# An adaptive-layernorm block with a gated scan and a routed expert layer: weights loaded apart from rows, early scatters, one more block table, and a bias added by VectorE

## The chip, the cores and the metric

The kernel runs on one core of a Trainium2 chip. Five engines work beside each other, each through its own queue in order: TensorE (PE in the profile, with its weight loads as PEld), VectorE (DVE), ScalarE (ACT), GpSimd (POOL) and SyncE (SP). The metric is the device time of one execution in microseconds; lower is better. The time before is the median of nine runs, 473.71 us.

## The reference

`x` holds 32 sequences of 256 tokens with 128 features, 8192 tokens in all. Cut to what matters:

```python
mod = (silu(c) @ wmod).reshape(32, 6, 1, -1)
sa, ca, ga, sb, cb, gb = (mod[:, i] for i in range(6))
ga = (2 * (ga >= 0) - 1) * maximum(abs(ga), 0.25)       # gb likewise
h = layernorm(x) * (1 + ca) + sa
g, a, v = sigmoid(h @ Wg.T + bg), sigmoid(h @ Wd.T + bd), h @ Wv.T + bv
x = x + ga * g * scan(h_t = a_t * h_{t-1} + (1 - a_t) * v_t)
h = layernorm(x) * (1 + cb) + sb
probs = softmax(h @ gate_w.T + gate_b)                  # 8 experts
gate = probs where among the two largest, else 0
y = relu(h @ w1[e] + b1[e]) @ w2[e] + b2[e]             # for each expert e
x = x + gb * sum_e gate[:, e] * y[:, e]
```

Here `w1[e]` is 128 x 512 and `w2[e]` is 512 x 128. Only the two chosen experts of a token have a weight other than zero, so the kernel computes two pairs (token, expert) for each token.

## The kernel before

**Supertiles.** The 8192 tokens are cut into 16 supertiles (`s`) of 512 tokens, each four tiles of 128. A supertile goes through four steps: `a_norm` (first layernorm), `a_mix` (three products, gates and the scan), `a_res` (residual and second layernorm) and `a_route` (router, ranks, and the rows to send). The string `HEAD` lays out the first six rounds; after it a round does one step of each of four supertiles. The step letters are n, m, r and R.

**Scatter by expert.** `a_route` writes each token's normalised row twice into `rw` (once for each chosen expert), followed by its gate value and the number of the place its result belongs to: `RW = D + 2` words (L69). It finds the row's place within its expert's region by ranks, counted with products against triangular and all-one matrices (L423, L425) and written as indices `pi` (L439). Eight indirect DMAs a supertile, issued by GpSimd, scatter the rows into `reg` in HBM (L447). They aren't issued at once: `drip` (L461) takes one or two of them from the list `sending` after each step and each block, and makes each wait for the last ScalarE instruction of that step or block. The tile `rw` and the indices `pi` have three buffers.

**Blocks.** A block is 256 rows of one expert. How many blocks are full after a supertile depends on the data; what is sure is a lower bound, `full(s)`. At the supertiles in `TAKE` a `table` is computed on VectorE (L471 to L520) that lists expert and place of the next blocks; 45 are listed by the tables up to supertile 12, and the last table, after supertile 15, lists the rest of the 71. Blocks of a table are held back (`held`) until the rows of its supertile have been sent.

**A block's work** is three steps, each in another `b_step`, so that three blocks are in flight:
- `b_load` (L533): SyncE reads expert and place from the table into registers (L535, L536), loads the block's rows `xr` (130 KB, waiting for the sixteen scatters issued last) and then the expert's first weights and bias `ww` (514 KB, five buffers). It runs `LOOK = 4` blocks ahead.
- `b_in` (L547): PE transposes the rows (L551), ScalarE and VectorE split them into a high and a low part (L553, L554).
- `b_up` (L557): twelve products (L566 to L568), then four ReLUs with bias; in the first `HA = 53` blocks one of the four is done by VectorE (L572), the rest by ScalarE (L574).
- `b_down` (L578): PE reads the expert from the table (L581), puts the second bias into the accumulator by a product of ones with the bias's two parts (L584), and adds sixteen products (L587). The accumulator `pby` has one buffer. ScalarE copies it out as `yt`, scaled by the gate value that came with the rows (L591); `yt` has eight buffers (`YTB`). Two indirect DMAs from GpSimd scatter `yt` into `yd`, in the order of tokens (L593).

**Final sums.** When the blocks up to a certain one are done, `c_load` (L600) loads the two results of every token of a supertile into `yk` (two buffers), and `c_add` (L610), up to three supertiles behind (`CLAG`), adds them, multiplies by the row of `gb` that PE spreads over partitions (L614, L621), adds `x` (L622) and stores (L623). The supertiles up to `CUT` are ready together, at a block of the last table.

**Order.** The four steps carry priorities (`AHEAD`), and a scheduler orders each engine's instructions when the kernel is built; within an engine nothing overtakes. All loads and stores of the main part are issued by SyncE, all scatters by GpSimd.

Of the kernel before, what the change touches and what calls it, by code (L numbers as in the profile page):

```python
# [11 lines left out]
I32 = mybir.dt.int32  # L12
# [14 lines left out]

TAKE = (2, 3, 4, 5, 6, 7, 8, 10, 12)
CUT = 9

# [12 lines left out]

HA = 53

# [9 lines left out]
def adaln_moe(ctx: ExitStack, tc: tile.TileContext, x, Wg, bg, Wv, bv, Wd, bd,  # L55
# [12 lines left out]
    NJ = BLK // P  # L68
    RW = D + 2  # L69

# [30 lines left out]
    gbb = cp.tile([P, E], F32, name="gbb")  # L101
    b2r = cp.tile([E, D], F32, name="b2r")
    for s in range(1, XE):
# [6 lines left out]
    nc.gpsimd.dma_start(gbb, gate_b.partition_broadcast(P))  # L110
    nc.gpsimd.dma_start(b2r, b2)
    ones_f = cp.tile([P, P], F32, name="ones_f")
# [4 lines left out]
    nc.gpsimd.affine_select(tri, ones_b, pattern=[[1, P]], compare_op=ALU.is_gt, fill=0.0, base=0, channel_multiplier=-1)  # L117
    ones_r = cp.tile([2, P], F32R, name="ones_r")
    nc.vector.tensor_copy(ones_r, ones_f[0:2, :])

# [92 lines left out]
    wr = cp.tile([P, E, H], F32, name="wr")  # L213
    b2w = cp.tile([K, E, D], F32R, name="b2w")
    b2s = cp.tile([E, 2, D], F32R, name="b2s")
    N3 = 3 * NB
# [3 lines left out]
    def late_constants():  # L220
        nc.vector.tensor_copy(b2s[:, 0], b2r)
        nc.vector.tensor_tensor(b2s[:, 1], b2r, b2s[:, 0], op=ALU.subtract)
        for h in range(2):
            nc.sync.dma_start(b2w[h:h + 1].bitcast(F32), b2s[:, h].bitcast(F32))

# [36 lines left out]
    nc.gpsimd.iota(padi, pattern=[[P, NJ]], base=K * N, channel_multiplier=1)  # L262
    nc.vector.tensor_copy(pad[:, :, D + 1].bitcast(I32), padi)

# [6 lines left out]
    tc.add_to_no_dep_group("fill", f.ins)  # L271

    mh = cp.tile([P, T, 1], F32, name="mh")
    nc.vector.memset(mh, -0.5)
# [110 lines left out]
    def a_route(a, base):  # L385
# [57 lines left out]
        nc.vector.reciprocal(rc, sm)  # L443
        nc.vector.tensor_tensor(rw[:, :, :, D], e8[:, :, 0:K], rc.unsqueeze(2).to_broadcast([P, T, K]), op=ALU.mult)
        nc.gpsimd.tensor_copy(rw[:, :, :, D + 1].bitcast(I32), dst[:, s * T:(s + 1) * T])
        def send(j, k):
# [5 lines left out]

        sending.extend((s, send, j, k) for j in range(T) for k in range(K))
        return rk[:, T]

# [3 lines left out]
    held = []  # L459

    def drip(n, behind):  # L461
        for _ in range(min(n, len(sending))):
            s, send, j, k = sending.pop(0)
            w = send(j, k)
            tc.add_manual_dep(w, behind.ins.name, WAIT, reason="pace of the rows on their way out")
            sent.append(w)
            if not sending or sending[0][0] != s:
                while held and held[0][0] <= s:
                    blocks.extend(held.pop(0)[1])

# [61 lines left out]

    def b_load(n, tb, i):  # L533
        with tc.issue_after(loaded[-1].ins) if loaded else nullcontext():
            e = nc.sync.value_load(tb[i:i + 1, 0:1], min_val=0, max_val=E - 1)  # L535
            r = nc.sync.value_load(tb[i:i + 1, 1:2], min_val=0, max_val=E * CAP)  # L536
        xr = bk.tile([P, NJ, RW], F32, tag="xr", name=f"xr{n}", bufs=YTB + 6)
        w = nc.sync.dma_start(xr, reg[bass.ds(r, BLK)].rearrange("(t p) d -> p t d", p=P))
        tc.add_to_no_dep_group("rows", w.ins)
        for x in sent[-2 * K * T:]:  # L540
            tc.add_manual_dep(w.ins, x.name, WAIT, reason="its rows")
        ww = bk.tile([P, WW], F32, tag="ww", name=f"ww{n}", bufs=5)
        b = dict(n=n, xr=xr, ww=ww, tb=tb, i=i)
        loaded.append(nc.sync.dma_start(ww, wd[bass.ds(e, 1)].rearrange("o p f -> p (o f)")))
        return b

# [10 lines left out]
    def b_up(b):  # L557
        n, xs, ww = b["n"], b["xs"], b["ww"]
        hh = bk.tile([P, NH, BLK], F32, tag="hh", name=f"hh{n}")
        for k0 in range(0, NH, 2):  # L560
# [8 lines left out]
            for k in (k0, k0 + 1):  # L569
                bias = ww[:, O_B1 + k:O_B1 + k + 1]  # L570
                if k % 4 == 1 and n < HA:
                    nc.vector.tensor_scalar(hh[:, k], p1[:, k - k0], bias, 0.0, op0=ALU.add, op1=ALU.max)  # L572
                else:
                    w = nc.scalar.activation(hh[:, k], p1[:, k - k0], AF.Relu, bias=bias)  # L574
                    b.setdefault("last", w)
        b["hh"] = hh

    def b_down(b):  # L578
        n, xr, hh, i = b["n"], b["xr"], b["hh"], b["i"]
        py = psb.tile([P, 512], F32, tag="pby", name=f"pby{n}")[:, :NJ * D]  # L580
        e = nc.tensor.value_load(b["tb"][i:i + 1, 0:1], min_val=0, max_val=E - 1)  # L581
        we = wr[:, bass.ds(e, 1), :].rearrange("p o f -> p (o f)")
        b2t = b2w[:, bass.ds(e, 1), :].to_broadcast([2, NJ, D])
        nc.tensor.matmul(py.rearrange("p (j d) -> p j d", d=D), ones_r, b2t, start=True, stop=False)  # L584
        for j in range(NJ):
            for k in range(NH):
                nc.tensor.matmul(py[:, j * D:(j + 1) * D], hh[:, k, j * P:(j + 1) * P], we[:, k * D:(k + 1) * D],  # L587
                                 start=False, stop=(j == NJ - 1 and k == NH - 1))
        yt = bk.tile([P, NJ, D], F32, tag="yt", name=f"yt{n}", bufs=YTB)
        for j in range(NJ):  # L590
            nc.scalar.activation(yt[:, j], py[:, j * D:(j + 1) * D], AF.Copy, scale=xr[:, j, D:D + 1])  # L591
        for j in range(NJ):
            w = nc.gpsimd.indirect_dma_start(  # L593
                out=yd, out_offset=bass.IndirectOffsetOnAxis(ap=xr[:, j, D + 1:D + 2].bitcast(I32), axis=0),
                in_=yt[:, j], in_offset=None, bounds_check=K * N - 1, oob_is_err=False)
# [14 lines left out]
    def c_add(s, yk, step):  # L610
# [5 lines left out]
        for j0 in range(0, T, step):  # L616
            js = slice(j0, j0 + step)
            nc.vector.tensor_tensor(ot[:, js], yk[:, 0, js], yk[:, 1, js], op=ALU.add)
            for q in range(j0 // JB, (j0 + step) // JB):
# [10 lines left out]
    nload = 0  # L630
    LOOK = 4

    def b_step():

        nonlocal nload
# [48 lines left out]
    for t, todo in enumerate(steps):  # L684
        def step3(s):
            nonlocal base, done
            with tc.high_priority(AHEAD[3] * (s >= EARLY)):
# [11 lines left out]
                elif s == NS - 1:  # L699
# [65 lines left out]
```

## Time and profile before

| | |
|---|---|
| median of nine runs | 473.71 us (472.88 to 478.02) |
| profiled execution | 477.95 us, of which the span from first to last instruction is 476.2 us |
| busy share of the span | PE 86%, weight loads 73%, VectorE 60%, ScalarE 61%, GpSimd 61% |
| mean granted PE clock | 0.913 of full speed |
| scatters of rows (L447) | 128, 981 ns each |
| scatters of results (L593) | 142, 994 ns each |
| bias products (L584) | 71, 384 ns each (pipelined) |
| DMA | 91.5 MB, 192 GB/s over the span |

The span's row is the length between the first and the last instruction of the profiled execution. A line of the windows gives a stretch in us from the start of the span, then the busy time of each engine in it. A line of a timeline gives the start, the duration, the engine, the line of the kernel, the operation, the tile it writes and the tiles it reads, and in brackets how long the engine sat idle before it and what ended that. Matmuls overlap, so that the distance between two starts tells more than a duration.

### The profile page before, as it was taken

The page shows a single profiled execution, that of the slowest core. Times are in us where ns is not written, and L with a number is a line of the kernel's source. Part 1 is how long each engine was busy: PE and PEld are TensorE (multiplying, and loading weights), DVE is VectorE, ACT ScalarE, POOL GpSimd, SP SyncE. Part 2 cuts the span into 40 slices and gives each one's busy share as a digit, 9 for nine tenths or more (in the row PEclk, how much of TensorE's full clock was granted, in tenths as well). Part 3 has the DMA queues.
Part 4 walks back from the last instruction along what each step waited for, and adds up shares of the span by engine and source line. Part 5 has one row for each costly group of instructions (what it writes and reads, how often), then busy time and mean ns, then how long its engine had stood idle before and what let it go on. Part 6 is the DMA issues. An engine that isn't in the chain of part 4 may idle for free.

```text
span 476.2 us, 11399 instructions
## 1 busy us (share of the span) xinstructions
PE 409.7 (86%) x2810; PEld 346.6 (73%) x2810; DVE 285.1 (60%) x1511; ACT 291.4 (61%) x726; POOL 291.5 (61%) x322
## 2 busy tenths in 40 slices
PE   4757665779999999998996999999769999799980
PEld 3224433468988988987886999899669999699970
DVE  6899999968987886883884445122013214444464
ACT  4766654768979877965763666555326566446640
POOL 3633755536777777777677777777754445334551
PEclk9985758779999999998997999999959999889996
DMA  7997211183737656555543767885189869999773
GB/s 194 329 308 252 85 39 40 45 285 88 232 102 229 178 160 206 143 167 140 156 141 104 232 192 211 204 241 166 50 263 274 249 207 289 303 301 330 226 216 112
DMA packets 81845, 91.52 MB, mean 192 GB/s; under 512 B 8577, under 2 KB 66408, under 8 KB 81782
## 3 DMA queue, kind: packets, MB, share of 16 engines
q1 hardware_dynamic: 73024, 73.84, 54.5%
q0 software_dynamic: 8704, 16.94, 10.3%
q8 instruction: 26, 0.43, 0.4%
q14 instruction: 37, 0.30, 0.2%
q10 hardware_dynamic: 54, 0.02, 0.0%
HBM read 64.24 MB, written 27.43 MB: 192 GB/s over the span
## 4 chain that ended last, share of the span: by engine, by line
PE 67%; DVE 12%; DMA 9%; issue 4%; ACT 2%; POOL 2%; SPq 2%; POOLq 0%; ACTq 0%; DVEq 0%
PE pby L587 28%; PE p L566 7%; PE p L567 7%; PE p L568 7%; PE pz L346 5%; PE pby L584 4%; PE pbx L551 3%; DMA yd<-yt,xr 2%; DMA reg<-rw,pi 2%; DVE sta L280 2%; DMA yk<-yd 2%; PE pl L397 2%; DMA ww<-wd 2%; PE po L374 2%; DMA xa<-in_L_attn_x_dram 1%
## 5 line engine op out<-in xcount | busy, mean ns | idle before, releaser
L593 POOL DMA_INDIRECT yd<-yt,xr x142 | 141.1, 994 | 93.0 <-ACT yt L591 55.6
L447 POOL DMA_INDIRECT reg<-rw,pi x128 | 125.6, 981 | 50.3 <-issue 22.5
L587 PE MATMUL pby<-wr,hh 128*128 x1136 | 154.1, 289 | 0.0
L587 PEld LDWEIGHTS pby<-wr,hh 128*128 128x128 f32 x1136 | 139.7, 199 | 9.4 <-issue 0.9
L574 ACT ACTIVATE hh<-p,ww 128x256 f32<-128x256 f32 x231 | 97.8, 476 | 19.8 <-PE p L568 11.9
L591 ACT ACTIVATE yt<-pby,xr 128x128 f32<-128x128 f32 x142 | 45.0, 365 | 84.1 <-PE pby L587 84.0
L566 PE MATMUL p<-xs,ww 128*128 128x256 f32 x284 | 89.2, 315 | 4.5 <-DMA ww<-wd 3.9
L554 DVE TENSOR_TENSOR xs<-pbx,xs 128x256 fp32r<-128x256 f32 x71 | 29.9, 421 | 101.3 <-ACT xs L553 100.8
L568 PE MATMUL p<-xs,ww 128*128 128x256 f32 x284 | 81.6, 288 | 0.0
L567 PE MATMUL p<-xs,ww 128*128 128x256 f32 x284 | 81.4, 287 | 0.0
L346 PE MATMUL pz<-h,wT 128*128 128x512 f32 x96 | 56.2, 704 | 8.9 <-ACT tg L361 3.5
L566 PEld LDWEIGHTS p<-xs,ww 128*128 128x128 f32 x284 | 54.9, 194 | 6.3 <-issue 4.2
L567 PEld LDWEIGHTS p<-xs,ww 128*128 128x128 f32 x284 | 55.3, 195 | 0.7 <-issue 0.7
L568 PEld LDWEIGHTS p<-xs,ww 128*128 128x128 f32 x284 | 55.0, 194 | 0.2 <-issue 0.2
L346 PEld LDWEIGHTS pz<-h,wT 128*128 128x128 f32 x96 | 19.5, 231 | 24.9 <-issue 9.9
L551 PE MATMUL pbx<-ident,xr 128*128 128x128 f32 x142 | 28.4, 283 | 5.9 <-DMA xr<-reg 5.9
L324 ACT ACTIVATE xn<-xa,nra,nya 128x128 f32<-128x128 f32 x64 | 26.4, 489 | 10.1 <-DVE nra L307 10.1
L572 DVE TENSOR_SCALAR hh<-p,ww 128x256 f32<-128x256 f32 x53 | 25.4, 478 | 11.5 <-ACT hh L574 9.5
L553 ACT ACTIVATE xs<-pbx 128x256 fp32r<-128x256 f32 x71 | 27.6, 388 | 7.0 <-PE pbx L551 7.0
L584 PE MATMUL pby<-b2w,ones_r 2*128 x71 | 27.2, 384 | 2.0 <-ACT yt L591 2.0
L402 ACT ACTIVATE rw<-pb 128x1024 f32<-128x1024 f32 x16 | 16.4, 1023 | 19.6 <-DMA reg<-rw,pi 5.9
L382 ACT ACTIVATE xm<-xa,nrb,nyb 128x128 f32<-128x128 f32 x64 | 26.4, 484 | 1.4 <-DVE nrb L307 1.3
(181 smaller groups left out, 574.7 us busy)
## 6 DMA issues: line engine op xcount, KB each, us to landing
ww<-wd SPq DMA_DIRECT2D x71, 514.0 KB
xr<-reg SPq DMA_DIRECT2D x71, 130.0 KB
yk<-yd SPq DMA_DIRECT2D x30, 256.0 KB
wd<-wh SPq DMA_DIRECT2D x8, 514.0 KB
xa<-in_L_attn_x_dram SPq DMA_DIRECT2D x16, 256.0 KB
out_dram<-ot SPq DMA_DIRECT2D x15, 256.0 KB
yd<-yt,xr POOLq DMA_INDIRECT x142
w1s<-in_L_ffn_w_dram SPq DMA_DIRECT2D x8, 256.0 KB
```

The costliest lines, as they stand in the source:

```text
L346: nc.tensor.matmul(z, wT[:, i], h1, start=True, stop=True)
L447: w = nc.gpsimd.indirect_dma_start(out=reg, out_offset=bass.IndirectOffsetOnAxis(ap=pi[:, j * K + k:j * K + k + 1], axis=0), in_=rw[:, j, ...
L551: nc.tensor.transpose(px[:, j * P:(j + 1) * P], xr[:, j, 0:D], ident)
L554: nc.vector.tensor_tensor(xs[:, 1], px, xs[:, 0], op=ALU.subtract)
L566: nc.tensor.matmul(z, hi, xs[:, 0], start=True, stop=False)
L567: nc.tensor.matmul(z, hi, xs[:, 1], start=False, stop=False)
L568: nc.tensor.matmul(z, lo, xs[:, 0], start=False, stop=True)
L574: w = nc.scalar.activation(hh[:, k], p1[:, k - k0], AF.Relu, bias=bias)
L584: nc.tensor.matmul(py.rearrange("p (j d) -> p j d", d=D), ones_r, b2t, start=True, stop=False)
L587: nc.tensor.matmul(py[:, j * D:(j + 1) * D], hh[:, k, j * P:(j + 1) * P], we[:, k * D:(k + 1) * D], start=False, stop=(j == NJ - 1 and k = ...
L591: nc.scalar.activation(yt[:, j], py[:, j * D:(j + 1) * D], AF.Copy, scale=xr[:, j, D:D + 1])
L593: w = nc.gpsimd.indirect_dma_start(out=yd, out_offset=bass.IndirectOffsetOnAxis(ap=xr[:, j, D + 1:D + 2].bitcast(I32), axis=0), in_=yt[:, ...
```

## The change

- Rows are one word shorter (`RW = D + 1`): the gate value no longer travels with them. It is kept in a tile `gate` for all tokens, and the final sum scales both results with it: ScalarE the first (four instructions a supertile), VectorE the second within the sum (four instead of one).
- The second bias is no longer a product. `b2b` holds it for all experts on all partitions; in `b_down` VectorE reads the expert from the table and writes `yt` as accumulator plus bias. The products of a block start the accumulator themselves.
- All four ReLUs of a block are done by ScalarE; `HA` is gone.
- `b_load` is split: `b_weights` reads the expert and loads `ww`, `LOOKW = 4` blocks ahead; `b_rows` reads the place and loads `xr`, `LOOKR = 2` blocks ahead. The rows' wait is for the sixteen scatters that were the last when the block was released.
- The scatters of the first three supertiles (`EARLY = 3`) are all issued at the end of `a_route` and wait for no other instruction; `drip`'s rule for later ones is simpler.
- A table at supertile 13 is added (`TAKE`), so that 49 blocks are listed before the last table; `CUT` goes from 9 to 11.

The core of the diff:

```diff
-TAKE = (2, 3, 4, 5, 6, 7, 8, 10, 12)
-CUT = 9
+TAKE = (2, 3, 4, 5, 6, 7, 8, 10, 12, 13)
+CUT = 11
...
-HA = 53
+LOOKW = 4
+LOOKR = 2
...
-    RW = D + 2
+    RW = D + 1
...
-    b2r = cp.tile([E, D], F32, name="b2r")
+    b2b = cp.tile([P, E, D], F32, name="b2b")
...
     def late_constants():
-        nc.vector.tensor_copy(b2s[:, 0], b2r)
-        nc.vector.tensor_tensor(b2s[:, 1], b2r, b2s[:, 0], op=ALU.subtract)
-        for h in range(2):
-            nc.sync.dma_start(b2w[h:h + 1].bitcast(F32), b2s[:, h].bitcast(F32))
+        nc.sync.dma_start(b2b.rearrange("p e d -> p (e d)"), b2.rearrange("e d -> (e d)").partition_broadcast(P))
...
+    gate = cp.tile([P, NS, T, K], F32, name="gate")
...
-        nc.vector.tensor_tensor(rw[:, :, :, D], e8[:, :, 0:K], rc.unsqueeze(2).to_broadcast([P, T, K]), op=ALU.mult)
-        nc.gpsimd.tensor_copy(rw[:, :, :, D + 1].bitcast(I32), dst[:, s * T:(s + 1) * T])
+        nc.vector.tensor_tensor(gate[:, s], e8[:, :, 0:K], rc.unsqueeze(2).to_broadcast([P, T, K]), op=ALU.mult)
+        nc.gpsimd.tensor_copy(rw[:, :, :, D].bitcast(I32), dst[:, s * T:(s + 1) * T])
...
         sending.extend((s, send, j, k) for j in range(T) for k in range(K))
+        if s < EARLY:
+            drip(len(sending), None)
...
+    def release():
+        while held and not (sending and sending[0][0] <= held[0][0]):
+            blocks.extend((tb, q, ends, len(sent)) for tb, q, ends in held.pop(0)[1])
 
     def drip(n, behind):
...
-            tc.add_manual_dep(w, behind.ins.name, WAIT, reason="pace of the rows on their way out")
+            if behind:
+                tc.add_manual_dep(w, behind.ins.name, WAIT, reason="pace of the rows on their way out")
             sent.append(w)
-            if not sending or sending[0][0] != s:
-                while held and held[0][0] <= s:
-                    blocks.extend(held.pop(0)[1])
+            release()
...
-    def b_load(n, tb, i):
+    def b_weights(n, tb, i):
         with tc.issue_after(loaded[-1].ins) if loaded else nullcontext():
             e = nc.sync.value_load(tb[i:i + 1, 0:1], min_val=0, max_val=E - 1)
+        ww = bk.tile([P, WW], F32, tag="ww", name=f"ww{n}", bufs=5)
+        loaded.append(nc.sync.dma_start(ww, wd[bass.ds(e, 1)].rearrange("o p f -> p (o f)")))
+        return dict(n=n, ww=ww, tb=tb, i=i)
+
+    def b_rows(b):
+        n, tb, i = b["n"], b["tb"], b["i"]
+        with tc.issue_after(loaded[-1].ins):
             r = nc.sync.value_load(tb[i:i + 1, 1:2], min_val=0, max_val=E * CAP)
         xr = bk.tile([P, NJ, RW], F32, tag="xr", name=f"xr{n}", bufs=YTB + 6)
         w = nc.sync.dma_start(xr, reg[bass.ds(r, BLK)].rearrange("(t p) d -> p t d", p=P))
         tc.add_to_no_dep_group("rows", w.ins)
-        for x in sent[-2 * K * T:]:
+        for x in b["sent"]:
             tc.add_manual_dep(w.ins, x.name, WAIT, reason="its rows")
-        ww = bk.tile([P, WW], F32, tag="ww", name=f"ww{n}", bufs=5)
-        b = dict(n=n, xr=xr, ww=ww, tb=tb, i=i)
-        loaded.append(nc.sync.dma_start(ww, wd[bass.ds(e, 1)].rearrange("o p f -> p (o f)")))
-        return b
+        loaded.append(w)
+        b["xr"] = xr
...
-                if k % 4 == 1 and n < HA:
-                    nc.vector.tensor_scalar(hh[:, k], p1[:, k - k0], bias, 0.0, op0=ALU.add, op1=ALU.max)
-                else:
-                    w = nc.scalar.activation(hh[:, k], p1[:, k - k0], AF.Relu, bias=bias)
-                    b.setdefault("last", w)
+                w = nc.scalar.activation(hh[:, k], p1[:, k - k0], AF.Relu, bias=bias)
+                b.setdefault("last", w)
...
-        b2t = b2w[:, bass.ds(e, 1), :].to_broadcast([2, NJ, D])
-        nc.tensor.matmul(py.rearrange("p (j d) -> p j d", d=D), ones_r, b2t, start=True, stop=False)
         for j in range(NJ):
             for k in range(NH):
                 nc.tensor.matmul(py[:, j * D:(j + 1) * D], hh[:, k, j * P:(j + 1) * P], we[:, k * D:(k + 1) * D],
-                                 start=False, stop=(j == NJ - 1 and k == NH - 1))
+                                 start=(k == 0), stop=(k == NH - 1))
         yt = bk.tile([P, NJ, D], F32, tag="yt", name=f"yt{n}", bufs=YTB)
-        for j in range(NJ):
-            nc.scalar.activation(yt[:, j], py[:, j * D:(j + 1) * D], AF.Copy, scale=xr[:, j, D:D + 1])
+        e = nc.vector.value_load(b["tb"][i:i + 1, 0:1], min_val=0, max_val=E - 1)
+        b2t = b2b[:, bass.ds(e, 1), :].to_broadcast([P, NJ, D])
+        nc.vector.tensor_tensor(yt, py.rearrange("p (j d) -> p j d", d=D), b2t, op=ALU.add)
...
             js = slice(j0, j0 + step)
-            nc.vector.tensor_tensor(ot[:, js], yk[:, 0, js], yk[:, 1, js], op=ALU.add)
+            for j in range(j0, j0 + step):
+                nc.scalar.activation(yk[:, 0, j], yk[:, 0, j], AF.Copy, scale=gate[:, s, j, 0:1])
+            for j in range(j0, j0 + step):
+                nc.vector.scalar_tensor_tensor(ot[:, j], yk[:, 1, j], gate[:, s, j, 1:2], yk[:, 0, j], op0=ALU.mult, op1=ALU.add)
...
-        while nload < len(blocks) and nload < i + 1 + LOOK:
-            tb, q, ends = blocks[nload]
-            blocks[nload] = b_load(nload, tb, q)
-            blocks[nload]["ends"] = ends
+        while nload < len(blocks) and nload < i + 1 + LOOKW:
+            tb, q, ends, n = blocks[nload]
+            blocks[nload] = b_weights(nload, tb, q)
+            blocks[nload].update(ends=ends, sent=sent[n - 2 * K * T:n])
             nload += 1
+        while nrows < nload and nrows < i + 1 + LOOKR:
+            b_rows(blocks[nrows])
+            nrows += 1
...
+                release()
...
-            drip(2 if t < len(steps) - NS or len(sending) > K * T else 1, st[s]["last"])
+            drip(2 if len(sending) > K * T else 1, st[s]["last"])
```

More of the change, by code (lines that the diff above doesn't have):

```diff
@@ L110, in adaln_moe @@
     nc.gpsimd.dma_start(gbb, gate_b.partition_broadcast(P))
-    nc.gpsimd.dma_start(b2r, b2)
     ones_f = cp.tile([P, P], F32, name="ones_f")
@@ L117, in adaln_moe @@
     nc.gpsimd.affine_select(tri, ones_b, pattern=[[1, P]], compare_op=ALU.is_gt, fill=0.0, base=0, channel_multiplier=-1)
-    ones_r = cp.tile([2, P], F32R, name="ones_r")
-    nc.vector.tensor_copy(ones_r, ones_f[0:2, :])
     def iota_f(name, n, step):
@@ L213, in adaln_moe @@
     wr = cp.tile([P, E, H], F32, name="wr")
-    b2w = cp.tile([K, E, D], F32R, name="b2w")
-    b2s = cp.tile([E, 2, D], F32R, name="b2s")
     N3 = 3 * NB
@@ L262, in adaln_moe @@
     nc.gpsimd.iota(padi, pattern=[[P, NJ]], base=K * N, channel_multiplier=1)
-    nc.vector.tensor_copy(pad[:, :, D + 1].bitcast(I32), padi)
+    nc.vector.tensor_copy(pad[:, :, D].bitcast(I32), padi)
     def into_reg(ins, group):
@@ L587, in b_down @@
                 nc.tensor.matmul(py[:, j * D:(j + 1) * D], hh[:, k, j * P:(j + 1) * P], we[:, k * D:(k + 1) * D],
-                                 start=False, stop=(j == NJ - 1 and k == NH - 1))
+                                 start=(k == 0), stop=(k == NH - 1))
         yt = bk.tile([P, NJ, D], F32, tag="yt", name=f"yt{n}", bufs=YTB)
-        for j in range(NJ):
-            nc.scalar.activation(yt[:, j], py[:, j * D:(j + 1) * D], AF.Copy, scale=xr[:, j, D:D + 1])
+        e = nc.vector.value_load(b["tb"][i:i + 1, 0:1], min_val=0, max_val=E - 1)
+        b2t = b2b[:, bass.ds(e, 1), :].to_broadcast([P, NJ, D])
+        nc.vector.tensor_tensor(yt, py.rearrange("p (j d) -> p j d", d=D), b2t, op=ALU.add)
         for j in range(NJ):
             w = nc.gpsimd.indirect_dma_start(
-                out=yd, out_offset=bass.IndirectOffsetOnAxis(ap=xr[:, j, D + 1:D + 2].bitcast(I32), axis=0),
+                out=yd, out_offset=bass.IndirectOffsetOnAxis(ap=xr[:, j, D:D + 1].bitcast(I32), axis=0),
                 in_=yt[:, j], in_offset=None, bounds_check=K * N - 1, oob_is_err=False)
@@ L630, in adaln_moe @@
     nload = 0
-    LOOK = 4
+    nrows = 0
     def b_step():
-        nonlocal nload
+        nonlocal nload, nrows
         i = len(flow)
-        while nload < len(blocks) and nload < i + 1 + LOOK:
-            tb, q, ends = blocks[nload]
-            blocks[nload] = b_load(nload, tb, q)
-            blocks[nload]["ends"] = ends
+        while nload < len(blocks) and nload < i + 1 + LOOKW:
+            tb, q, ends, n = blocks[nload]
+            blocks[nload] = b_weights(nload, tb, q)
+            blocks[nload].update(ends=ends, sent=sent[n - 2 * K * T:n])
             nload += 1
+        while nrows < nload and nrows < i + 1 + LOOKR:
+            b_rows(blocks[nrows])
+            nrows += 1
         b = blocks[i] if i < len(blocks) else None
```

## The prediction

> **What bounds the kernel now.** I read the windows by stage first, then the timelines of TensorE (PE) and GpSimd (POOL) where PE stops, then the chain of waits. The stages (columns: length, busy us of PE, weight loads, VectorE, ScalarE, POOL, then PE clock, DMA share, GB/s):
>
> ```profile
> 0.00:100.00 100.00, 63.96 (x225) 37.00 (x226) 90.10 (x603) 62.25 (x131) 51.29 (x71) 0.78 0.55 165
> 100.00:200.00 100.00, 99.73 (x737) 85.80 (x737) 79.75 (x464) 81.55 (x204) 72.86 (x77) 0.98 0.60 176
> 340.00:360.00 20.00, 13.37 (x80) 12.23 (x81) 2.66 (x6) 5.37 (x16) 11.78 (x13) 0.74 0.69 207
> 400.00:420.00 20.00, 16.66 (x116) 15.21 (x115) 8.88 (x19) 8.18 (x24) 6.65 (x8) 0.85 1.00 302
> ```
>
> The chain that ended last:
>
> ```profile
> PE 67%; DVE 12%; DMA 9%; issue 4%; ACT 2%; POOL 2%; SPq 2%; POOLq 0%; ACTq 0%; DVEq 0%
> PE pby L587 28%; PE p L566 7%; PE p L567 7%; PE p L568 7%; PE pz L346 5%; PE pby L584 4%; PE pbx L551 3%; DMA yd<-yt,xr 2%; DMA reg<-rw,pi 2%; DVE sta L280 2%; DMA yk<-yd 2%; PE pl L397 2%; DMA ww<-wd 2%; PE po L374 2%; DMA xa<-in_L_attn_x_dram 1%
> ```
>
> Up to 100 VectorE is nearly full and PE is not; from 100 on PE is full except for holes, and at 400 the DMA share is 1.00. The chain gives PE 67% and the bias product 4%; taken alone, that would be the wrong reading. The holes come from POOL, whose 73% hides that its queue never rests:
>
> ```profile
> 340.09 0.98 POOL L593 DMA_INDIRECT yd<-yt,xr  x1 [0.30 <-ACT yt L591]
> 341.38 0.97 POOL L447 DMA_INDIRECT reg<-rw,pi  x1 [0.30 <-DMA yd<-yt,xr]
> 342.65 0.96 POOL L447 DMA_INDIRECT reg<-rw,pi  x1 [0.30 <-DMA yd<-yt,xr]
> ...
> 343.14 0.38 PE L584 MATMUL pby<-b2w,ones_r 2*128 x1 [0.72 <-ACT yt L591]
> 347.31 0.69 PE L551 MATMUL pbx<-ident,xr 128*128 128x128 f32 x2 [3.79 <-DMA xr<-reg]
> 350.06 0.55 PE L566 MATMUL p<-xs,ww 128*128 128x256 f32 x1 [2.06 <-DMA ww<-wd]
> ```
>
> A scatter starts every 1.27 us. From the first scatter of results at 108.63 to the end of the last scatter of rows at 343.6, POOL issues 179 scatters (210 in all by then, 128 of rows and 82 of results, less the 31 before): 235/179 = 1.313 us each, copies and gaps included. That is its limit; a supertile with three blocks needs 8 + 6 = 14 of them, 18.4 us, while PE's period there is 17.1 us (the products of L346 recur at 117.43, 134.61, 151.77). So POOL falls behind, buffers fill, PE stops at 216 and 247 to 258, and the last rows are late: all 45 blocks known by then are done and PE stands from 343 to 350.
>
> The start is late for the same queue:
>
> ```profile
> 71.36 0.95 POOL L447 DMA_INDIRECT reg<-rw,pi  x1 [2.60 <-ACT xm L382]
> 83.94 0.98 POOL L447 DMA_INDIRECT reg<-rw,pi  x1 [3.53 <-ACT rw L402]
> 88.44 0.95 POOL L447 DMA_INDIRECT reg<-rw,pi  x1 [2.16 <-ACT xm L382]
> ```
>
> Scatters of rows wait for ScalarE instructions put ahead of them as pace, though the indices of the first three supertiles exist at 48.5, 60.7 and 65.3 (L439). The 26th is issued at 90.96 and the first block's transposes run at 95.80.
>
> **The change, part by part.**
> *The bias product (L584) goes.* In a run of undisturbed blocks L584 starts at 371.38, 375.25, 379.19: 3.9 us a block; from L584 to the first L587 it is 0.31. A block becomes 3.59; 71 x 0.31 = 22 us of PE. Where POOL is the limit (100 to 340) this gives nothing, so I count 22 blocks after it, not 71.
>
> *Instead VectorE adds the bias* and reads the expert from the table. The add is 128x256 with one operand in PSUM, as L554 (0.421) is: 0.42. VectorE has no register load before. The nearest rows are SyncE's and PE's loads of the same table:
>
> ```profile
> L581 PEldq TENSOR_LOAD <-tb x71: 297/305/557, 67.9 to 327.3; - x71
> L535 SPq TENSOR_LOAD <-tb x71: 264/274/803, 67.2 to 436.2; - x71
> ```
>
> With the operation behind it (0.15) that is 0.43 on SyncE; from start to the end of its check it takes 0.82 (67.2 to 68.02) and on PE 0.92. So 0.43 to 0.92 a block, or nothing where it runs under the instruction before; I take 0.45. VectorE loses L572 (0.478) in 53 blocks: net 0.4 to 0.9 a block. It was 13.6 us busy a supertile (79.75 over 100/17.1 periods); three blocks make 14.8 to 16.3, under POOL's 18.4, which covers it. Without that cover it costs three times the net per supertile.
>
> The Trainium skill's "DMA: Bandwidth & Descriptors" (Latency and other measured facts) gives a floor of about 600 ns for a tensor_load, which speaks against 71 more of them; the rows here show 264 to 305 ns. By the page 71 loads are 43 us of VectorE, by the rows 19 to 22, and both stay hidden while POOL limits.
>
> *ScalarE:* it loses the scaled copies L591 (two back to back 0.63, 71 times: 45 us), gains L572's work (53 x 0.476 = 25) and 64 scalings in the final sum (four of L382's size back to back take 1.64: 26). About +6 in all; at 100 to 200 it falls. In the tail a step has four ReLUs (1.57), xs (0.39) and four scalings (1.64) = 3.6, as long as a PE block: no cover left there. The final sum on VectorE gets four 128x128 operations (L280 does four in 0.86) for one of 0.69: +0.2 to 0.4.
>
> *First three supertiles scattered at once.* 24 scatters without waits from 48.5: 24 x 1.27 plus 2.7 for the two instructions between them ends at 81.7; landing 2.3, load of rows 2.4 (345.06 to 347.31 does the same): first transposes at about 86.5 instead of 95.8. Weights are no longer behind the rows (their table exists at 68), so products follow at once; before, L566 waited 1.79 more. But in the built order the fourth supertile's ranks (L423, 85.98 before) now stand behind the first block's products, 12 at the slow clock's 0.21 = 2.5 us, and behind its ReLUs; its indices move from 87.5 to about 92.5 (bounds 87.5 and 97). From there POOL has 186 scatters to the last one of rows, the same 82 of results among them: 92.5 + 186 x 1.313 = 337 (332 to 342), not 343.6.
>
> *A table more.* 49 instead of 45 blocks are known before the last table, so PE has four blocks (14.4 us) to do while the last rows go out. Its cost is some 25 small VectorE operations of 0.16 us = 4 us around 270 to 290, under POOL. Weights for the last blocks now come before their rows: the wait for ww (2.06) goes. Rows are loaded two blocks ahead instead of four; SyncE's queue still puts the outputs and the loads of results, which wait for VectorE and for scatters, in front of them.
>
> *From the last row on:* last scatter starts at 336, lands at 338.3, transposes at 340.7, products at 341.5 (350.06 before). 22 blocks x 3.59 = 79 us: 420.5.
>
> *Final sums.* With CUT 11 the first result loads wait for block 56 (before: 52), about four blocks later in the work that is left. While weights, rows, loads and outputs run together a step moves 0.53 + 0.13 + 0.52 + 0.26 = 1.44 MB. At 302 GB/s (400 to 420) that is 4.8 us, above PE's 3.59; the loads of results before were 4.9 apart (390.42 to 459.25, fourteen steps). Seven such steps in the built order: 7 x 1.2 = 8.4, and 2 for the first, which waits for POOL's backlog: last block at 431 (463.24 before). The same skill page (Where 436 GB/s comes from) puts the HBM side at about 358 GB/s; no window here passes 329. By it a step is 4.0 and the seven give 3.0.
>
> After the last product six sums stand in PE's order instead of three. With two buffers for yk, load (3.5), scalings (1.6) and sum (0.3 of the first part, 1.45 of the rest before the output lets SyncE go on) come every 3 to 3.6 us, and the last needs 2.9 to land: 18.5 us, not 13 (463.24 to 476.2). Ends at 449.4.
>
> **The sum:** 476.2 - 8.6 (earlier products) - 15.6 (four blocks of 3.9 no longer behind) - 6.8 (22 x 0.31) - 1.4 (losses in the rest: 11.8 before, being 463.24 - 350.06 - 26 x 3.9, and 10.4 now) + 5.5 (tail) = 449.3. The profiled execution took 477.95, 1.75 more than its span of 476.2, and is 4.2 above the median of the runs, 473.71; I take the difference of the spans, 26.9, off the median: **447**.
>
> **Rivals.**
> *The tail takes more (0.17).* Rows two ahead are 7 us, and a load under full DMA took 5.74 (yk at 407.23). If every one of 14 blocks waits 1 us and the six sums go at 4.5: +14 + 6: 467. For it: 302 GB/s and ScalarE's 3.6. Against: before, 429 to 441 ran blocks at full PE with 329 GB/s.
>
> *POOL is no limit (0.08).* If PE keeps all 22 us and the hole closes too: 473.7 - 22 - 7 - 15.6 + 3 = 432 or below. Against it stand 179 scatters without rest.
>
> *VectorE becomes the bound (0.14, slower).* It waits in order for a product of PE (yt), with the chain of the next supertiles queued behind it, and the accumulator has one buffer. It decides once a block costs it 1.6 us net ((18.4 - 13.6)/3). Before's gain of 27 is gone over 13 supertiles at 2.1 more each, 2.3 us a block. At 2.7 a supertile takes 21.7: 447 + 13 x 3.3 = 490. For it: 97% VectorE from 20 to 80. Against: ScalarE did this waiting at 82% busy, and its queue was as strict.
>
> *It does nothing (0.04), 474:* losses after 341 give back the 27, that is 1.2 us in each of the 22 blocks beyond those counted.
>
> **How the numbers follow.** The likeliest case has 0.57 and 447. Its bounds: 332 for the last scatter, no first wait, the tail's 13 and 329 GB/s (4.4 a step) give 473.7 - 26.9 - 5 - 2 - 5.5 - 3 = 431; upward 342 and the tail rival give 472. Range 430 to 470, with VectorE's case, no change and part of the tail's left out above. About 0.5% (2.4 us) is what a measurement of this kernel tells from no change. Faster 0.82, same 0.04, slower 0.14.
>
> **What would show it.** Right: 24 scatters of rows without gaps from 48; first transposes near 86; last rows near 337 with no hole longer than 2 us after it; blocks of 3.6 us; DMA share 1.0 from 375 to 410; six sums after the last product. Wrong: VectorE above 95% between 100 and 290 and POOL resting there; transposes waiting for xr in the tail.

## The result and the profile after

| | before | after |
|---|---|---|
| median | 473.85 us (469.77 to 479.04, 31 runs) | 483.42 us (481.16 to 485.59, 10 runs) |
| ratio, 95% interval | | 1.0197 (1.0172 to 1.0223) |
| span of the profiled execution | 476.2 | 480.9 (the execution itself took 482.67) |

The changed kernel is 2% slower; 447 was forecast. In two sets of experiments the kernel before itself took 548 us; what was run in them is compared only within its set.

The windows of the changed kernel, cut as those of before (length; busy us of PE, weight loads, VectorE, ScalarE, POOL; PE clock, DMA share, GB/s):

```profile
0.00:100.00 100.00, 66.12 (x260) 39.33 (x261) 88.66 (x574) 61.13 (x130) 47.01 (x65) 0.80 0.61 189
100.00:200.00 100.00, 90.90 (x660) 78.69 (x659) 74.99 (x462) 76.53 (x180) 75.38 (x81) 0.93 0.53 160
...
340.00:360.00 20.00, 16.00 (x131) 14.84 (x129) 3.73 (x9) 8.29 (x21) 12.78 (x13) 1.00 0.70 209
...
400.00:420.00 20.00, 17.38 (x144) 16.20 (x142) 9.65 (x28) 11.68 (x35) 8.40 (x9) 1.00 0.91 262
```

VectorE is not the bound: 75% from 100 to 200, less than before. PE, which was full there, now has 9 us of holes. The hole at 340 is smaller than before (16.0 busy of 20 against 13.4), and yet the end comes later. The chain that ended last, which ran through PE for 67% before, now has it at 3%; its shares make only 38% of the span, so I take no more from it than that:

```profile
DMA 14%; issue 10%; POOL 6%; DVE 4%; PE 3%; ACT 1%; POOLq 0%; DVEq 0%; SPq 0%
```

To see where the forecast and the result part I cut the span at three events that every kernel here has: the start of the last scatter of rows, the second split of block 49 (the add that writes `xs` on VectorE, 70 being the last block), and the end of the last `yt`. All from the timelines (the forecast's second and third event are products, close beside). Each row is one profiled execution, so a difference of one or two us between rows means little:

| us | last scatter of rows starts | to block 49's split | to the last `yt` | to the end | span |
|---|---|---|---|---|---|
| before | 342.7 | 20.3 | 100.9 | 12.3 | 476.2 |
| forecast | 336 | 5.5 | 89.5 | 18.5 | 449.5 |
| after | 342.8 | 17.9 | 96.2 | 24.1 | 480.9 |
| rows four ahead (e8) | 339.4 | 11.7 | 90.9 | 20.0 | 462.0 |

All four terms were missed in the same direction: 6.8, 12.4, 6.7 and 5.6 us. The tail alone (24.1 against 12.3) outweighs all that was gained before it. The last row belongs to the experiment that explains most of the difference.

The first term, in the timeline of the changed kernel (start, duration, engine, line, operation, tiles, idle before it and what ended that):

```profile
81.88 1.03 POOL L442 DMA_INDIRECT reg<-rw,pi  x1 [0.30 <-issue]
82.91 0.21 POOL L440 COPY rw<-dst 128x8 int32<-128x8 int32 x1
...
86.45 0.69 PE L556 MATMUL pbx<-ident,xr 128*128 128x128 f32 x2 [3.95 <-DMA xr<-reg]
87.17 0.38 ACT L558 ACTIVATE xs<-pbx 128x256 fp32r<-128x256 f32 x1 [2.09 <-PE pbx L556]
87.45 0.22 ACT L426 ACTIVATE e<-d 128x32 f32<-128x32 f32 x1
...
93.67 0.19 PE L418 MATMUL pq<-mk,tri 128*128 128x40 bf16 x1
...
98.91 0.98 POOL L442 DMA_INDIRECT reg<-rw,pi  x1 [15.79 <-DVE nyb L298]
```

The 24 scatters wait for no pace (the one break of 4 us, behind the eighth, is two other instructions of POOL and 2.26 us until the next indices exist), and the first transposes come at 86.45, both as forecast. But PE stands 3.95 us for those transposes' rows with everything else behind them, and POOL then stands for 15.8 us: supertile 3's exponentials (L426) and ranks (L418, 93.67; 85.98 before) are behind block 0 in ScalarE's and PE's queues, and its indices exist only at 97.9. So all that the early scatters gained is lost again by the 25th (89.70 before).

The other terms, in the view of waits (waited for: us in total, times, longest):

```profile
PE pbx L556 <- DMA xr<-reg: 30.7, 19, 5.1
...
ACT yk L620 <- DMA yk<-yd: 18.2, 9, 4.7
PE gt L615 <- DVE ot L625: 17.4, 5, 6.8
```

PE waits 30.7 us for rows; before it was 5.9. The same view of SyncE's queue names what stands ahead of those rows (three lines of the changed kernel, then two of before, where L538 loads rows and L544 weights):

```profile
SPq L545 <- DMA reg<-rw,pi: 60.2, 14, 13.4
SPq L537 <- ACT hh L576: 48.4, 41, 4.8
SPq L537 <- PE p L573: 45.8, 33, 3.5
...
SPq L538 <- DMA reg<-rw,pi: 150.5, 34, 14.0
SPq L544 <- ACT hh L574: 5.9, 14, 0.9
```

L537 is the load of weights. In these two lines it waits 94 us for one of its five buffers, and the rows (L545) are queued behind it. Before, the queue stood for the scatters instead. In the run of undisturbed blocks (changed kernel, timeline):

```profile
378.08 0.35 SPq L537 DMA_DIRECT2D ww<-wd  x1
379.27 0.38 SPq L545 DMA_DIRECT2D xr<-reg  x1
379.45 0.38 PE L556 MATMUL pbx<-ident,xr 128*128 128x128 f32 x2
381.57 0.35 SPq L537 DMA_DIRECT2D ww<-wd  x1
382.75 0.38 SPq L545 DMA_DIRECT2D xr<-reg  x1
383.23 0.41 PE L556 MATMUL pbx<-ident,xr 128*128 128x128 f32 x2 [0.77 <-DMA xr<-reg]
```

The rows issued at 379.27 are transposed at 383.23, 3.96 us later, and PE had to wait for them. Weight buffers are freed by PE's products and ScalarE's ReLUs, rows come behind the weights, and products need the rows: a loop as long as a block. Blocks 49 to 60 come 3.88 us apart ((403.4 - 360.7)/11), where 3.59 was forecast and 3.93 stood before ((390.4 - 362.9)/7 in blocks 49 to 56, ahead of the first load of results; 4.07 up to block 60). That this loop sets the pace is a reading of these lines so far; e8 and e16 test it.

### The profile page after: what moved, and what is told of

It reads as the page before. It is cut to its first block, busy times and chain, and to the rows that moved or that the text cites. A ratio compares the mean times of both kernels' runs of the same rounds, so it can differ in the third digit from the quotient of the medians.

```text
span 480.9 us, 11244 instructions
## 1 busy us (share of the span) xinstructions
PE 382.1 (79%) x2739; PEld 328.9 (68%) x2739; DVE 294.0 (61%) x1591; ACT 287.9 (60%) x701; POOL 293.0 (61%) x321
## 5 line engine op out<-in xcount | busy, mean ns | idle before, releaser
L442 POOL DMA_INDIRECT reg<-rw,pi x128 | 127.1, 993 | 59.1 <-issue 25.1
L587 PE MATMUL pby<-wr,hh 128*128 x1136 | 149.2, 279 | 3.6 <-issue 1.9
L576 ACT ACTIVATE hh<-p,ww 128x256 f32<-128x256 f32 x284 | 114.3, 476 | 40.0 <-PE p L573 18.9
L571 PE MATMUL p<-xs,ww 128*128 128x256 f32 x284 | 88.4, 321 | 4.4 <-ACT xs L558 3.1
L592 DVE TENSOR_TENSOR yt<-pby,b2b 128x256 f32<-128x256 f32 x71 | 29.9, 422 | 64.1 <-PE pby L587 56.3
L556 PE MATMUL pbx<-ident,xr 128*128 128x128 f32 x142 | 29.1, 288 | 31.9 <-DMA xr<-reg 30.7
L556 PEld LDWEIGHTS pbx<-ident,xr 128*128 128x128 f32 x142 | 16.8, 144 | 40.4 <-issue 14.0
L620 ACT ACTIVATE yk<-yk,gate 128x128 f32<-128x128 f32 x64 | 20.7, 393 | 24.5 <-DMA yk<-yd 18.2
L341 PEld LDWEIGHTS pz<-h,wT 128*128 128x128 f32 x96 | 18.9, 226 | 23.9 <-issue 9.7
L622 DVE SCALAR_TENSOR_TENSOR ot<-yk,gate 128x128 f32<-128x128 f32 x64 | 18.7, 346 | 18.9 <-DMA out_dram<-ot 9.8
```

The costliest lines, as they stand in the source:

```text
L341: nc.tensor.matmul(z, wT[:, i], h1, start=True, stop=True)
L442: w = nc.gpsimd.indirect_dma_start(out=reg, out_offset=bass.IndirectOffsetOnAxis(ap=pi[:, j * K + k:j * K + k + 1], axis=0), in_=rw[:, j, ...
L556: nc.tensor.transpose(px[:, j * P:(j + 1) * P], xr[:, j, 0:D], ident)
L571: nc.tensor.matmul(z, hi, xs[:, 0], start=True, stop=False)
L592: nc.vector.tensor_tensor(yt, py.rearrange("p (j d) -> p j d", d=D), b2t, op=ALU.add)
L622: nc.vector.scalar_tensor_tensor(ot[:, j], yk[:, 1, j], gate[:, s, j, 1:2], yk[:, 0, j], op0=ALU.mult, op1=ALU.add)
```

## The experiments

**One part alone (e1 to e4).** The kernel before with one of the four parts of the diff each: the hunks of `RW`, `b2b`, `gate`, the ReLUs and the final sum (e1), of `EARLY` in `a_route` and `drip` (e2), of `TAKE` and `CUT` (e3), of `b_weights`, `b_rows`, `LOOKW` and `LOOKR` (e4), as they stand above.

> The kernel before with only the bias moved to VectorE and the gate into the final sum; scatters, table and loads as before. Theory (GpSimd's queue sets the time of the last scatter of rows, VectorE has room): last scatter of rows unchanged at 343 (+-3), the 26 blocks after it 0.31 us shorter each, the final sums a little longer: 466 to 470 against 473.8. Rival (VectorE, with a register load and an add for each block, holds the others up): last scatter of rows later than 348 and 478 or more.

> The kernel before with only the first three supertiles' scatters issued at once. Theory (the first block's transposes then stand in TensorE's queue ahead of the fourth supertile, and GpSimd runs dry until its indices come): GpSimd idle more than 8 us after its 24th scatter, last scatter of rows within 3 us of 343, time 471 to 477. Rival (early scatters are a gain by themselves, and it is other parts that lose it): last scatter of rows at 336 or earlier, time 464 to 468.

> The kernel before with only the added table and CUT 11. Theory (GpSimd, not a lack of listed blocks, is what TensorE waits for at the end of the scatters, and the final sums come four blocks later): the hole near 343 no more than 3 us shorter, six sums after the last product, time 476 to 484. Rival (four more listed blocks fill the hole): no stop longer than 3 us after the last scatter, time 460 to 468.

> The kernel before with only the weights loaded apart, rows two blocks ahead. Theory (rows two ahead come late when GpSimd or the DMA is late): TensorE waits for xr 15 us or more in all (before: 6), time 476 to 483. Rival (two ahead is enough, and weights ahead of rows save 2 us after the last scatter): 470 to 474.

| | us | ratio to before | last scatter of rows | tail after the last `yt` |
|---|---|---|---|---|
| e1 bias | 485.31 | 1.0205 (1.0153 to 1.0257) | 351.6 | 15.8 |
| e2 early scatters | 473.14 | 0.9957 (0.9934 to 0.9980) | 340.9 | 11.8 |
| e3 table and CUT | 475.15 | 1.0004 (0.9978 to 1.0030) | 341.7 | 19.0 |
| e4 loads apart | 476.06 | 1.0038 (0.9993 to 1.0082) | 344.1 | 11.8 |

By the expectations, e1 has the time and the late last scatter of its rival. e2 has what its theory said: POOL idle for 16.7 us after its 24th scatter. e3 is in neither range: its stretch from the last scatter to block 49 is 12.9 us, 7.4 shorter than before, where the theory allowed 3. e4 just reaches its theory's time, but not its sign, with 9.5 us of waits for rows where 15 were named.

The four effects add up to +2.0%, and so does the whole; that looks as if the bias part were the culprit and the rest neutral. It isn't so, as e8 shows. e1 loses its time before the blocks: its last scatter of rows is nine us late,

```profile
351.58 0.96 POOL L440 DMA_INDIRECT reg<-rw,pi  x1 [0.30 <-issue]
```

and the delay is there before the first block, so it isn't the rival's register load and add in each block: the 24th scatter starts at 97.0 instead of 88.4, the first block comes at 107.2 instead of 96.7. In the changed kernel, which sends the first rows at once, that loss isn't there (342.8). So the same 10 us have another cause in each of the two. Why e1 starts late was not tried apart; its build has another order of VectorE's work in the first 60 us. e3 shows both halves of the table: the last `yt` ends 10 us earlier (453.7, before 463.9; 47 blocks are split at the last scatter of rows, before 45), and the tail, with its sums begun four blocks later, grows by 6.7.

**One thing undone in the changed kernel (e5 to e8).**

```diff
 e6    the four scalings and four scalar_tensor_tensor of c_add:
+            nc.vector.tensor_tensor(ot[:, js], yk[:, 0, js], yk[:, 1, js], op=ALU.add)
 e7    the register load and the add of b_down:
+        nc.scalar.activation(yt, py.rearrange("p (j d) -> p j d", d=D), AF.Copy)
 e8
-LOOKR = 2
+LOOKR = 4
```

> The changed kernel with the bias part undone (product, scaled copies, one ReLU of four on VectorE, gate with the rows). If the four parts are independent it loses the bias part's ten us: 473 to 475. If the bias part costs only because of the early shift it makes in the kernel before (last scatter of rows 351.6 there, 342.8 in the changed kernel), nothing of that is left to win here, and it stays above 479.

> The changed kernel with the gate values left out of the final sum (no scalings by ScalarE, one plain add by VectorE); the output lacks the gates. Theory: the scalings wait for yk at the head of ScalarE's queue (18.2 us in nine waits in the changed kernel), in front of the ReLUs of the next blocks, and lengthen the tail: 472 to 477, with the tail after the last results below 20 us (24.5 in the changed kernel). Rival: the tail is set by loads of results, and the loss sits with VectorE in the blocks: 481 or more.

> The changed kernel with yt copied out by one ScalarE instruction of 256 columns and the second bias left out (no register load and no add on VectorE). Theory of the final sums: about the same, 480 to 485. Rival, VectorE's in-order wait for the product and its register load: 474 to 478, and the waits of VectorE for pby (56 us in the changed kernel) are gone with PE's holes.

> The changed kernel with LOOKR = 4. If rows loaded two ahead come late by themselves (PE waits 26.8 us for them), it gains 4 us or more: 479 or less. If they wait for GpSimd's queue, which is full until 343 either way, it stays within 2 us of the changed kernel, 481 to 486, and the waits of PE for xr from 100 to 340 stay above 10 us.

| | us | ratio to before |
|---|---|---|
| changed kernel | 483.42 | 1.0197 (1.0172 to 1.0223) |
| e5 bias part undone | 476.60 | 1.0030 (0.9997 to 1.0064) |
| e6 no gates in the sum | 478.63 | 1.0065 (1.0016 to 1.0114) |
| e7 copy by ScalarE, no second bias | 480.35 | 1.0123 (1.0050 to 1.0195) |
| e8 rows four ahead | 465.17 | 0.9815 (0.9768 to 0.9862) |

One constant turns a loss of 2.0% into a gain of 1.9%: e8 beats both kernels. Its time is that of the first expectation; e5 and e6 lie between their two ranges. SyncE's waits in e8:

```profile
SPq L545 <- DMA reg<-rw,pi: 113.3, 37, 13.7
...
SPq L537 <- ACT hh L576: 10.9, 17, 1.2
...
SPq L537 <- PE p L573: 6.1, 6, 4.1
```

and a stretch of its timeline:

```profile
377.48 0.38 PE L556 MATMUL pbx<-ident,xr 128*128 128x128 f32 x2
378.37 0.39 SPq L545 DMA_DIRECT2D xr<-reg  x1
380.26 0.35 SPq L537 DMA_DIRECT2D ww<-wd  x1
380.90 0.38 PE L556 MATMUL pbx<-ident,xr 128*128 128x128 f32 x2
381.45 0.53 SPq L545 DMA_DIRECT2D xr<-reg  x1
383.68 0.35 SPq L537 DMA_DIRECT2D ww<-wd  x1
384.34 0.38 PE L556 MATMUL pbx<-ident,xr 128*128 128x128 f32 x2
```

The waits for weight buffers fall from 94 to 17 us. The transposes come 3.43 us apart without a wait; those at 384.34 use rows issued at 374.88, 9.5 us earlier, where it was 3.96. But the rows' own waits for scatters rise from 60 to 113 us. PE's waits for rows show where the lead counts (changed kernel from 100 to 340 and from 340 on, then e8 the same):

```profile
PE pbx L556 <- DMA xr<-reg: 17.5, 9, 5.1
PE pbx L556 <- DMA xr<-reg: 9.3, 9, 1.7
...
PE pbx L556 <- DMA xr<-reg: 21.0, 8, 6.4
PE pbx L556 <- DMA xr<-reg: 2.9, 1, 2.9
```

Up to 340 rows wait for POOL either way, as the second expectation had it (above 10 us); from there on the longer lead takes the waits away. By the table of the span e8 wins in all terms: 3.4 us at the last scatter of rows, 6.1 in the blocks around it (47 blocks split by then, 45 in the changed kernel), 5.3 in the run of blocks, 4.1 in the tail: 18.9. Of the 3.4, 1.6 are there at the end of the 24th scatter (82.91 and 81.29), before a block runs. Which stall behind SyncE's queue makes the tail shorter was not taken apart.

e6 prices the gates in this kernel: without them the tail is 18.0 us (24.1 with them), and the whole is 1.3% faster. One of e7's four executions took 1976.55 us; the others lie between 478.15 and 482.18, with 478.53 in the middle; 480.35 is in its first range, 478.53 in neither. e7 gains 0.7% with intervals that meet (from nothing to 1.5%); ScalarE takes over the copy there, so it shows only that VectorE's wait for the product is not all of the 2%.

**Rows two ahead, but first in the queue (e16).**

```diff
     def b_step():
+        while nrows < nload and nrows < i + 1 + LOOKR:
+            b_rows(blocks[nrows])
+            nrows += 1
         while nload < len(blocks) and nload < i + 1 + LOOKW:
```

> As e14: the changed kernel with LOOKR = 2 kept, but in each step the rows issued ahead of the weights, against a kernel before of about 474. Theory: rows two ahead are late because they stand in SyncE's queue behind a load of weights that waits for one of its five buffers; then most of the 18 us come back: 464 to 472, and a block takes 3.4 to 3.5 us from block 50 to 60 (3.9 in the changed kernel). Rival: two blocks are too short a lead whatever stands ahead: 478 to 485.

476.94 us, ratio 1.0053 (1.0017 to 1.0089): neither expectation. Blocks 49 to 60 are 3.40 us apart ((398.8 - 361.4)/11), as in e8, so the loop through the weight buffers is what slowed that run. The tail is short again too (19.1). But only 6.5 of the 18 us come back. By the spans 13.2 us are missing against e8: 6.3 at the last scatter of rows (345.7), 4.0 from there to block 49 (15.7) and 3.8 between block 60 and the last `yt` (57.3, in e8 53.5), with the tail 0.9 shorter. Of the 6.3, 2.1 are there at the end of the 24th scatter, and two more scatters of results (84, in e8 82) stand ahead of the last one of rows. PE's waits for rows don't tell the two kernels apart (e16, then e8):

```profile
PE pbx L556 <- DMA xr<-reg: 22.8, 9, 7.9
...
PE pbx L556 <- DMA xr<-reg: 26.8, 10, 6.4
```

So the place in the queue is one cost, and it is shown. That the lead of two blocks is another while POOL paces the rows fits with 45 blocks split at the last scatter of rows, as in the changed kernel, against 47 with rows four ahead; it is not shown, as the order on POOL and on SyncE differs as well.

**The bias part with rows four ahead (e17).** e8 with the bias part undone.

> As e13: the changed kernel with the bias part undone and LOOKR = 4, against a kernel before of about 474. With rows four ahead the changed kernel took 465.2, with the bias undone and rows two ahead 476.6. Theory: the bias part is worth 6 to 11 us once the rows don't set the pace, so undoing it gives 471 to 476. Rival: rows four ahead give the 18 us by themselves and the bias part is worth nothing: 463 to 467.

466.10 us, ratio 0.9873 (0.9825 to 0.9921), against 0.9815 (0.9768 to 0.9862) with the bias part: the intervals overlap, and the rival holds. What the part gains and gives back is seen in the terms: from the last scatter of rows to the last `yt` e17 takes 108.6 us and e8 102.7, so 5.9 us are won by the missing products, all of them in blocks 49 to 60 (3.96 us a block against 3.40). But the last scatter of rows starts at 336.1 in e17 and at 339.4 in e8, 3.3 us earlier: 0.6 by the end of the 24th scatter, 2.0 in POOL's stop behind it (13.8 against 15.8) and 0.8 over the 186 scatters from there. Undoing the bias part in the changed kernel gains 7 us, and here nothing that can be measured: with rows two ahead a block without the product (3.88) is hardly faster than with it (4.05 in e5), and the longer tail (24.1 against 19.3 in e5) remains to be paid. With rows four ahead the tails are alike (20.0 and 19.8).

**Blocks held back (e18).** e8, and no step of blocks is placed before supertile 3's scatters are listed.

```diff
-        if slot % SKIP and len(blocks) - len(flow) > BACK:
+        if slot % SKIP and len(blocks) - len(flow) > BACK and len(sent) + len(sending) > EARLY * K * T:
```

> As e15: the changed kernel with LOOKR = 4 and no step of blocks placed before the scatters of supertile 3 are listed, against a kernel before of about 474. Theory: GpSimd stands still from 82.9 to 98.9 because block 0 is ahead of supertile 3's ranks in PE's queue; without that supertile 3's indices come at 86 to 90, the last scatter of rows starts at 328 to 334, and the time is 456 to 461. Rival: the first blocks start as much later as the scatters start earlier, and the holes only move: 463 to 468.

470.15 us, ratio 0.9959 (0.9910 to 1.0007): slower than e8, and both expectations fell. Supertile 3's ranks come earlier (90.34 on PE), but then its indices are made late (VectorE, timeline of e18):

```profile
91.74 0.18 DVE L428 TENSOR_TENSOR rk<-pq,rk 128x40 f32<-128x40 f32 x1
91.86 0.73 DVE L353 SCALAR_TENSOR_TENSOR ta<-pz,cols,ta 128x512 f32<-128x512 f32 x1
...
93.10 1.25 DVE L360 TENSOR_TENSOR_SCAN hs<-aa,ta 128x256 f32<-128x256 f32 x2
...
94.83 0.67 DVE L361 SCALAR_TENSOR_TENSOR hs<-tg,hs 128x512 f32<-128x512 f32 x1
...
95.81 0.15 DVE L434 CAST pi<-pf 128x8 int32<-128x8 f32 x1
```

From `rk` to `pi` it is 4.1 us, with another supertile's gates and scan in between; before it was 1.0 (86.50 to 87.48). POOL still stands 13.6 us, and the first block comes at 102.9 instead of 87.2. The stop is made by VectorE's order as much as by the blocks. The last scatter of rows starts at 346.1, 6.7 later than in e8, although the 25th starts 0.3 earlier; what happens between was not taken apart.

**CUT (e12).** e18's kernel with `CUT = 9`, run in a set in which before took 547.66.

```diff
-CUT = 11
+CUT = 9
```

> The kernel of blocks held with CUT = 9. With CUT 11 twelve supertiles, with CUT 9 ten become ready together after the first eight blocks of the last table. If the choice of CUT shapes the tail, the number of sums after the last product changes and the time moves by 2 us or more against the run with CUT 11; if the tail is set by sixteen sums that start at block 57 in either case, it stays within 2 us.

561.51 (1.0265, 1.0209 to 1.0321), with CUT 11 in the same set 563.08 (1.0294, 1.0225 to 1.0364): no difference that can be told. The sums start after the first eight blocks of the last table either way (61 blocks are split before the first load of results in both).

The kernels of e16, e17 and e18 ran in the two sets with 548 us as well. Against before, the first had 1.0419 and 1.0369 (e10, e14), the second 1.0104 and 1.0062 (e9, e13), the third 1.0294 and 1.0244 (e11, e15). That is 2 to 4% worse than the 1.0053, 0.9873 and 0.9959 told above, and the record doesn't show why. So what is won or lost here is shown for sets in which before takes 474 us; e8 was not run in the others.

## Why the prediction was wrong, step by step

- **The bound: right.** POOL's scatters pace the kernel until the last rows are out. From 98.9 to the end of the last one at 343.8 there are 186 in 244.9 us, 1.317 each (1.313 forecast).
- **First three supertiles at once: mechanism right, size wrong.** Scatters without gaps (done at 82.9, forecast 81.7), first transposes at 86.45 (86.5). The indices of supertile 3 were put "from 87.5 to about 92.5 (bounds 87.5 and 97)"; they came at 97.9. I counted block 0's twelve products ahead of them, and they were; not counted were PE's 3.95 us of waiting for block 0's rows, VectorE's 2.31 for a product of the next supertile behind them (L369), and 2.6 on VectorE from the ranks (95.30) to the indices. The block's own products came at 90.41 and not at once. With that 6.4 of the 6.8 us of the first term are gone.
- **A table more, with rows two ahead: the step that failed.** "PE has four blocks (14.4 us) to do while the last rows go out" holds only if their rows are in. That "rows are loaded two blocks ahead instead of four" stood beside it without a cost; the rival of the tail priced it (7 us of lead), but only for the tail and as a mishap. The runs show 18 us in its place: 483.4 with rows two ahead, 465.2 with four (e8). It costs around the last scatter of rows (45 blocks split where 49 were counted, 47 in e8), in the run of blocks (3.88 us a block where 3.59 was counted, 3.40 in e8) and in the tail (24.1, in e8 20.0). The wait was new and named a resource I had not looked up: five weight buffers, with rows behind them in one queue. The size belongs to the combination of parts: without the bias part the shorter lead costs 10.5 us (e5 against e17), and in the kernel before, alone, 0.4% with an interval that takes in none (e4).
- **What rows four ahead leave open.** e8's span is still 12.5 us above the forecast, 6.2 of them between the last scatter of rows and block 49, where 47 blocks are split and not 49. e3, with the table alone and rows four ahead, has the same 47 and 12.9 us. The rows of block 47 go out only at 339.71 in e8, and PE waits 2.88 us for them; why so late was not tried.
- **Rows to follow the weights.** Weights before rows saves the one wait of 2.06, as counted; the price of the same reversal in every other step is what e16 measures: 6.5 us.
- **The bias product: a gain, half given back.** 6.8 us were counted after the last scatter of rows; e8 against e17 shows 5.9 there, and a loss of 3.3 before it, which I had at zero ("under POOL's 18.4, which covers it"). Over the 186 scatters which that cover was for it holds to 0.8 us; 2.0 of the loss are in POOL's stop before them. From 3.96 (e17) to 3.40 us a block it is more than the 0.31 forecast, for a reason not shown, but only for blocks 49 to 60, and only e8 and e16 get it.
- **VectorE becomes the bound (0.14, 490): near in time, wrong in kind.** VectorE's busy share from 100 to 200 is 75%, and e7, which takes away its waits for the product (56.3 us), gains 0.7%.
- **The register load: the rows held.** It takes 307 ns on VectorE (300 to 553) plus 183 for the operation behind it, 0.49 in all, where 0.45 was taken. The Trainium skill's "DMA: Bandwidth & Descriptors" (Latency and other measured facts) has a floor of about 600 ns; no run here shows one.
- **Final sums: right mechanism, too small.** 18.5 us forecast, 24.1 measured. The later start with the table is 6.7 of the growth (e3), the gates 6.1 (e6); 5.5 was counted for both. ScalarE's scalings, put at 1.6 us a sum without a wait, waited 18.2 us for `yk` at the head of its queue. With rows four ahead the tail is 20.0 with the gates and 19.8 with the whole bias part undone (e17), near the forecast; so most of the 6.1 seems to belong to the late rows, though e8 without the gates alone was not run.
- **Two readings of before.** PE's stop "247 to 258" lasts from 254.4 to 258.4 only, and a window does pass 329 GB/s (331 from 20 to 30). No term of the sum rests on either.

## What to carry to other kernels

A prefetch distance belongs to every block of a loop, so a shorter one has to be checked against the whole of the loop: what stands ahead of the load in its queue, which buffer that waits for, and which engine frees it. If the answer leads back to the engine that the load feeds, the loop has a floor, and removing work from that engine gains little until the floor is gone (here 0.17 us a block with the loop, 0.55 without). Effects of parts measured alone can add up to the whole by accident; only an undoing in the changed kernel showed which part cost the time there.

## What the runs showed of the hardware

TensorE's granted clock doesn't follow its busy share alone. From 280 to 340 PE is 82% busy both in the changed kernel (first line) and in e16 (second); the clock is 0.97 in the first, where no hole is longer than 1.9 us, and 0.87 in the second, with three holes of 2.3 to 3.2 us:

```profile
280.00:340.00 60.00, 48.90 (x385) 45.60 (x384) 14.30 (x66) 24.95 (x64) 46.07 (x48) 0.97 0.69 201
280.00:340.00 60.00, 49.09 (x365) 47.05 (x363) 15.38 (x74) 23.81 (x62) 46.05 (x48) 0.87 0.65 178
```

GpSimd's scatter of 128 rows takes nearly the same time with rows of 129 words (993 ns) as with 130 (981).
